# Five small edits to the order and the queues of a one-core, four-part transformer kernel

## The chip, the cores and the metric

The kernel runs on one core of one Trainium2 chip. A core has five engines that each work through their own list of instructions in order: TensorE (PE in the profile, with its weight loads as PEld), VectorE (DVE), ScalarE (ACT), GpSimd (POOL) and SyncE (SP). They meet only at semaphores. Transfers between memories are issued by an engine's queue (here SP's and ACT's, written SPq and ACTq) and carried out by 16 DMA engines. The metric is the device time of one execution in microseconds, as the median of several runs. All data are float32 except some weight codes.

## The reference

Two layers act in turn on an activation `x` of shape (2, 512, 256). Each has an attention and a feed-forward part, and each part is wrapped in two norms:

```python
x = x + layernorm(attn0(layernorm(x)))    # 16 heads of 128, rope, causal softmax, residual inside
x = x + layernorm(ffn0(layernorm(x)))     # gelu(x Wg) * (x Wu), then Wd; weights in 4-bit codes, 2048 wide
x = x + layernorm(attn1(layernorm(x)))    # linear attention: running sums of k and of k*v
x = x + layernorm(ffn1(layernorm(x)))     # silu(x Wg) * (x Wu), then Wd; weights from a 16-entry table, 688 wide

# inside attn0, for each of 2 sequences and 16 heads
q, k = rope(q + bq), rope(k + bk)
attn = softmax(where(causal, -inf, q @ k.T / sqrt(128)))
o    = attn @ v
```

## The kernel before, in words

The 1024 rows of `x` are held in on-chip memory for the whole run, as two sequences of four tiles of 128 rows. The first layer's attention is a loop over 32 "heads" (2 sequences of 16 heads), one call of `slot(i)` for each, with two more calls at the end. The other three parts work on four units `u` of two tiles each.

**The start.** The four tiles of the first sequence come in as four transfers: the two first ones from SP's queue, the two others from ACT's, behind a small transfer of bias columns (`cols_sb`). SP's queue then issues the weights of q and k, the rope tables (`cos_sb`, `sin_sb`), the weights of v, and more. `first_norms(0, 0.0)` computes the statistics of tile after tile on VectorE, the factors on GpSimd, and the normed tiles on ScalarE (tiles 0 and 1) and VectorE (tiles 2 and 3, `centred`). TensorE transposes each tile; ScalarE copies the result with the affine factors into `xT0`, in two halves of two tiles. `project("q", 0)` is done in two halves for that reason. Then come k of head 0, values, and q of head 1.

**A slot.** In `slot(i)` TensorE does, in this order: the scores of head i (4 matrix products), the projections of q and k of head i+1, the output projection of head i-2 (`projected_out`), a values projection where one is due, `attended(i - 1)` (probabilities of head i-1 times values), and later another values projection. In the slots 0 and 1 the values projection stands ahead of `attended`. VectorE takes the score rows out of PSUM with their minimum, ScalarE takes the exponentials and scales them by the inverse sums, and `turned_p(i)` transposes the probabilities: VectorE turns 32 x 32 blocks into the tile `turned`, and four transfers put its four groups of 32 partitions together into `pT`. There is one `turned` and one `pT` (`bufs=1`): `turned_p(i)` can write `turned` only when the transfers of head i-1 have read it, and the transfers can write `pT` only when `attended(i - 1)` has read it. For head 0 alone two of the four transfers are issued by ACT's queue; for all others SP's queue issues the four.

A projection (`project`) is four matrix instructions into one PSUM buffer of a pair (tag `mm`), then for q of a head above 1 three VectorE operations (one into `ra`, two into `rr`) and a GpSimd addition into `qT`; for k of such a head ScalarE and GpSimd take the place of the first of these.

**The norms.** `norms(u, y, stage, to)` ends each of the three first parts for unit u. For both tiles it computes the statistics of `y`, adds the normed `y` to `x`, computes the statistics of the new `x` (`stats` gives `rstd` and `shift`, whose last steps are small GpSimd operations), and lets ScalarE write the normed copy of `x` into a tile `n`. The copy is then turned into the layout that the next part needs: by VectorE and four transfers, or, for the last unit of the last part (stage 3) only, by four TensorE transposes and two ScalarE copies.

**The order.** It is fixed while the program is built. Norms and other side work are generators, and a small planner with a rough cost model decides after which step of TensorE each is continued: `yield until(a, b)` gives the planner's estimate of the time until `a` and `b` are written, and `poll()`, called after every step, continues what is due by the planner's clock. So a `yield` in a generator is a place where its instructions may fall behind others in every engine's list.

**The end.** The last tile of the last unit goes through a shorter path in `written`, and its result is stored as two transfers of 64 rows each, one from SP's queue and one from ACT's. All other output tiles are stored as one transfer of 128 rows from SP's queue.

Most engine operations show the line of a helper (L181 for all of VectorE, ScalarE and GpSimd, L163 for transfers, L272 and L278 for TensorE's products and transposes), so the trace is read by tile names.

Of the kernel before, what the change touches and what calls it, by code (L numbers as in the profile page):

```python
# [19 lines left out]
P = 128  # L20
# [12 lines left out]
HT = 2  # L33
# [155 lines left out]
def sandwich_kernel(  # L189
# [92 lines left out]
    def until(*aps):  # L282

        return max(0.0, times.written(*aps) - now[0])
# [3 lines left out]
    cols_sb = const.tile([P, 3 * NH + 2 * NK], F32, name="cols_sb")  # L288
    scalar.dma_start(out=cols_sb, in_=cols)
    for t in range(NT):  # L290
        (scalar if t >= HT else sync).dma_start(
            out=x0[0][:, t, :], in_=x[0][t * P : (t + 1) * P, :]
        )
    cos_sb = const.tile([P, S], F32, name="cos_sb")
# [47 lines left out]
    def norms(u, y, stage, to, eps=EPS, strided=False):  # L342

        x = [xs[u][:, j, :] for j in range(HT)]
        first = [stats(t, eps) for t in y]
        second = []
        for j in range(HT):
            yield until(first[j][0])  # L350
            add_scaled(x[j], y[j], first[j][0])
            second.append(stats(x[j], EPS))
        yield until(*(t for f in second for t in f))
        n = acts.tile([P, HT, D], F32, tag="ln", name=f"ln{stage}_{u}")


        by_blocks = (u, stage) != (NUNIT - 1, 3)
        for j in range(HT):
            rstd, shift = second[j]
            to_n, from_x = n[:, j, :], x[j]  # L360
            if not by_blocks:
                to_n = to_n.rearrange("p (k f c) -> p k f c", k=NK, c=4)
                from_x = from_x.rearrange(
                    "p (c f k) -> p k f c" if strided else "p (k c f) -> p k f c", k=NK, c=4
                )
            elif strided:
                to_n = to_n.rearrange("p (k m) -> p k m", k=NK)
                from_x = from_x.rearrange("p (m k) -> p k m", k=NK)
            scalar.activation(to_n, from_x, AF.Identity, bias=shift, scale=rstd)
        yield until(n)  # L370
        if by_blocks:

            tr = acts.tile([P, 4, NK, HT, 32], F32, tag="ln", name=f"tr{stage}_{u}")
            for j in range(HT):
                vector.transpose(
                    tr[:, :, :, j, :], n[:, j, :].rearrange("p (k c f) -> p c k f", k=NK, c=4)
                )
            for a in range(4):
                sync.dma_start(
                    out=to[:, a].rearrange("p k j t -> p (k j t)"),  # L380
                    in_=tr[32 * a : 32 * a + 32].rearrange("f c k j t -> f c (k j t)"),
                )
        else:
            pt = bank("t")
            for kc in range(NK):
                for j in range(HT):
                    transpose(
                        pt[:, kc * TU + j * P : kc * TU + (j + 1) * P],
                        n[:, j, kc * P : (kc + 1) * P],
                    )  # L390
            for kc in range(NK):
                scalar.copy(
                    to[:, :, kc].rearrange("p a j t -> p j a t"),
                    pt[:, kc * TU : (kc + 1) * TU].rearrange("p (j a t) -> p j a t", j=HT, a=4),
                )
        for j in range(HT):
            scalar.activation(x[j], x[j], AF.Identity, bias=first[j][1])
        yield until(to)
# [100 lines left out]
    with ExitStack() as at:  # L499
# [54 lines left out]
        def first_norms(b, wait):  # L554
# [138 lines left out]
            out=mask,  # L693
            in_=mask,
# [84 lines left out]
            rs[i] = small.tile([P, NT], F32, tag="rs", name="rs")  # L779
            vector.reciprocal(rs[i], sums[i])  # L780

        def project(kind, i, tag="mm"):
            b, h = divmod(i, NH)
            gg, hh = divmod(i, HG)
            w = wts[kind, gg]
            bias = col(kind, h)
            a = qk.tile([P, S], F32, tag="ra", name="ra")
            r = qk.tile([P, S], F32, tag="rr", name="rr")
            to = qk.tile([P, S], F32, tag=f"T{kind}", name=f"{kind}T")
            lo, hi = slice(0, 64), slice(64, 128)  # L790

            for cs in [slice(0, TU), slice(TU, S)] if (kind, i) == ("q", 0) else [slice(0, S)]:
                ps = bank(tag)
                for kc in range(NK):
                    matmul(
                        ps[:, cs],
                        w[:, kc, hh * DK : (hh + 1) * DK],
                        xT0[b][:, kc, cs],
                        kc == 0,
                        kc == NK - 1,  # L800
                    )
                if (kind == "k") == (i > 1) and i:
                    scalar.activation(a, ps, AF.Identity, bias=bias)
                    pool.tensor_mul(a, a, cos_sb)
                else:
                    vector.scalar_tensor_tensor(
                        a[:, cs], ps[:, cs], bias, cos_sb[:, cs], ALU.add, ALU.mult
                    )
                vector.scalar_tensor_tensor(
                    r[lo, cs], ps[hi, cs], bias[hi], sin_sb[hi, cs], ALU.add, ALU.mult  # L810
                )
                vector.scalar_tensor_tensor(
                    r[hi, cs], ps[lo, cs], bias[lo], sin_sb[lo, cs], ALU.add, ALU.mult
                )
            if (kind, i) == ("k", 1):
                inverted(0)
            (pool if i > 1 or kind == "q" else vector).tensor_add(to, a, r)
            (qT if kind == "q" else kT)[i] = to
# [51 lines left out]
        def turned_p(i):  # L870

            p, _ = ps_p.pop(i)
            for it in reversed(range(NT)):
                n = it + 1
                vector.transpose(
                    turned[:, :, 3 * it : 3 * it + n, :].rearrange("p j t b -> p t j b"),
                    p[:, p_at[it] : p_at[it] + n * P].rearrange("p (t j a) -> p t j a", t=n, j=4),
                )
            pT[i] = pr.tile([P, 4, 13, 32], F32, tag="pT", name="pT", bufs=1)
            for j in range(4):  # L880
                (scalar if i == 0 and j % 2 else sync).dma_start(
                    out=pT[i][:, j].rearrange("p t b -> p (t b)"),
                    in_=turned[32 * j : 32 * j + 32].rearrange("a j t b -> a j (t b)"),
                )
# [107 lines left out]
        def slot(i):  # L992
# [52 lines left out]
            else:  # L1045
                assert not terms
            for kind in "qk":
                if (kind, i) == ("q", 0):
                    pass
                elif i + 1 < NS:  # L1050
                    project(kind, i + 1)
                elif i <= NS:
                    next(main)
                    next(main)
                if kind == "q" and jobs and i % 2 == 0 and i >= 2:
                    dequantised(*jobs.popleft())
                if kind == "q" and i and now_in:
                    inverted(i)
            if now_in:
                p, _ = ps_p[i]  # L1060
# [5 lines left out]
            if i == 0:  # L1066
                values(0, 1, "t")
            elif i == 1:
                values(1, 1, "t")
            if 1 <= i < NS + 1:  # L1070
                attended(i - 1)
            if i == 0:
                values(1, 0)
            if now_in:
                turned_p(i)
            poll()
            if i < NS - HG:
                if i > 1:
# [193 lines left out]
    def written(u, j, y):  # L1272
        x = xs[u][:, j, :]
        row = ((u % 2) * HT + j) * P
        to = out[u // 2][row : row + P]
        if (u, j) != (NUNIT - 1, HT - 1):
            rstd, shift = stats(y, EPS)
            yield until(rstd, shift)
            add_scaled(x, y, rstd)
            vector.tensor_scalar(x, x, shift, None, ALU.add)  # L1280
            sync.dma_start(out=to, in_=x)
            return

        st = small.tile([P, 2, 6], F32, tag="st", name="st_last")
        mv = small.tile([P, 2], F32, tag="mv", name="mv_last")
        for c in range(2):
            vector.bn_stats(st[:, c, :], y[:, c * P : (c + 1) * P])
        vector.bn_aggr(mv, st)
        ve = small.tile([P, 1], F32, tag="ve", name="ve_last")
        vector.tensor_scalar(ve, mv[:, 1:2], EPS, None, ALU.add)  # L1290
        rstd = small.tile([P, 1], F32, tag="rstd", name="rstd_last")
        pool.tensor_tensor(rstd, ve, mhalf[:, :1], ALU.pow)
        centred = acts.tile([P, HT, D], F32, tag="ln", name="centred")[:, 0, :]
        vector.tensor_scalar(centred, y, mv[:, 0:1], None, ALU.subtract)
        add_scaled(x, centred, rstd)
        for engine, rows in ((sync, slice(0, P // 2)), (scalar, slice(P // 2, P))):
            engine.dma_start(out=to[rows], in_=x[rows])

    def run(work, steps=99):
        for _, _ in zip(range(steps), work):  # L1300
# [103 lines left out]
```

## Time and profile before

| What | us |
|---|---|
| Median of three runs (630.89 to 633.00) | 631.77 |
| The profiled execution, by its own time | 631.6 |
| Its span, from the first to the last instruction | 629.8 |
| TensorE busy in the span (98%) | 619.6 |
| VectorE busy (77%) | 487.7 |
| ScalarE busy (47%) | 298.2 |
| GpSimd busy (44%) | 277.8 |
| TensorE waiting for the transfers of `pT` (once) | 1.5 |
| TensorE waiting for tile `n` in the first norm (twice) | 1.3 |
| TensorE waiting for `ln` in the last norm (once) | 0.4 |

The span leaves out 1.8 us of the profiled execution that lie around it. The granted clock of TensorE is 0.998 of full speed. A row of the timeline is: start, duration, engine, line, operation, output and inputs with their sizes, count, and in brackets the engine's idle time before it with what ended it. In the list of waits a row gives who waited for what, then the total, the number of times and the longest. In the chain of work that ended last a row is start, duration, and the work.

### The profile page before, as it was taken

The page shows a single profiled execution, that of the slowest core. Times are in us where ns is not written, and L with a number is a line of the kernel's source. Part 1 is how long each engine was busy: PE and PEld are TensorE (multiplying, and loading weights), DVE is VectorE, ACT ScalarE, POOL GpSimd, SP SyncE. Part 2 cuts the span into 40 slices and gives each one's busy share as a digit, 9 for nine tenths or more (in the row PEclk, how much of TensorE's full clock was granted, in tenths as well). Part 3 has the DMA queues.
Part 4 walks back from the last instruction along what each step waited for, and adds up shares of the span by engine and source line. Part 5 has one row for each costly group of instructions (what it writes and reads, how often), then busy time and mean ns, then how long its engine had stood idle before and what let it go on. Part 6 is the DMA issues. An engine that isn't in the chain of part 4 may idle for free.

```text
span 629.8 us, 8201 instructions
## 1 busy us (share of the span) xinstructions
PE 619.6 (98%) x2504; PEld 461.7 (73%) x2504; DVE 487.7 (77%) x1154; ACT 298.2 (47%) x654; POOL 277.8 (44%) x350
## 2 busy tenths in 40 slices
PE   8999999999999999999999999999999999999996
PEld 5556666666666666666666778888888888888885
DVE  6869889878777989999988989779976372384843
ACT  4655666666655566656655661232313404415130
POOL 4254667546355375575666410350261151163341
PEclk9999999999999999999999999999999999999999
DMA  7366465474565656557453422211001001001000
GB/s 251 89 166 174 136 167 164 99 198 122 117 180 130 156 151 148 151 141 200 109 132 82 95 55 57 101 34 34 1 6 29 1 0 35 0 3 32 26 27 17
DMA packets 42444, 60.07 MB, mean 95 GB/s; under 512 B 5024, under 2 KB 29856, under 8 KB 42400
## 3 DMA queue, kind: packets, MB, share of 16 engines
q1 hardware_dynamic: 41600, 58.76, 35.7%
q10 hardware_dynamic: 800, 0.78, 0.5%
q8 instruction: 20, 0.33, 0.2%
q14 instruction: 24, 0.20, 0.1%
HBM read 28.33 MB, written 1.05 MB: 47 GB/s over the span
## 4 chain that ended last, share of the span: by engine, by line
PE 95%; DMA 2%; DVE 1%; issue 0%; ACT 0%; POOL 0%; ACTq 0%; POOLq 0%
PE ps_mm L272 38%; PE ps_o L272 22%; PE ps_s L272 21%; PE ps_t L272 14%; DMA pT<-turned 1%; DMA x<-in_x 1%; PE ps_t L278 0%; DVE turned L181 0%; DVE rr L181 0%; ACT ln L181 0%; POOL rstd L181 0%; ACTq L163 0%; DVE st L181 0%; DVE ra L181 0%; ACT p L181 0%
## 5 line engine op out<-in xcount | busy, mean ns | idle before, releaser
L181 POOL TENSOR_TENSOR wg<-wg,scratch 128x752 f32<-128x752 f32 x30 | 53.8, 1794 | 98.0 <-DVE scratch L181 98.0
L181 DVE SCALAR_TENSOR_TENSOR rr<-ps_mm,cols_sb,sin_sb 64x512 f32<-64x512 f32 (+1 forms) x126 | 93.4, 741 | 2.6 <-ACT ra L181 0.2
L181 ACT ACTIVATE p<-p,mn 128x512 f32<-128x512 f32 (+3 forms) x128 | 70.6, 552 | 31.3 <-DVE mn L181 31.3
L272 PE MATMUL ps_mm<-xT,wg 128*128 128x256 f32 (+1 forms) x352 | 84.9, 379 | 0.0
L272 PE MATMUL ps_s<-xT,wu 128*128 128x256 f32 x336 | 81.0, 379 | 0.0
L272 PE MATMUL ps_o<-wd,hT 128*128 128x256 f32 (+1 forms) x364 | 78.2, 372 | 0.0
L272 PE MATMUL ps_t<-pT,v 128*128 128x512 f32 (+3 forms) x256 | 74.3, 433 | 1.5 <-DMA pT<-turned 1.5
L272 PEld LDWEIGHTS ps_o<-wd,hT 128*128 128x128 f32 x364 | 67.4, 190 | 8.8
L272 PEld LDWEIGHTS ps_mm<-xT,wg 128*128 128x128 f32 (+1 forms) x352 | 66.4, 189 | 9.3 <-ACT ge L181 0.3
L272 PEld LDWEIGHTS ps_s<-xT,wu 128*128 128x128 f32 x336 | 63.8, 190 | 8.7
L272 PEld LDWEIGHTS ps_t<-pT,v 128*128 128x128 f32 x256 | 48.6, 190 | 28.9 <-issue 15.3
L181 DVE CUSTOM_DVE_ANT_0 p<-ps_s,mask 128x512 f32<-128x512 f32 (+2 forms) x96 | 45.9, 510 | 30.0 <-PE ps_s L272 29.9
L181 ACT ACTIVATE p<-p,rs 128x512 f32<-128x512 f32 (+3 forms) x128 | 61.4, 550 | 10.9 <-DVE rs L181 8.8
L272 PEld LDWEIGHTS ps_o<-wo,oT 128*128 128x128 f32 x256 | 48.6, 190 | 19.0 <-issue 13.6
L181 POOL TENSOR_TENSOR qT<-ra,rr 128x512 f32<-128x512 f32 x32 | 40.8, 1277 | 47.1 <-DVE rr L181 47.1
L272 PE MATMUL ps_s<-kT,qT 128*128 128x512 f32 (+2 forms) x192 | 60.9, 452 | 0.1
L272 PE MATMUL ps_o<-wo,oT 128*128 128x256 f32 x256 | 60.5, 379 | 0.0
L272 PE MATMUL ps_mm<-xT,wq 128*128 128x512 f32 (+1 forms) x128 | 58.4, 579 | 0.0
L272 PE MATMUL ps_mm<-xT,wk 128*128 128x512 f32 x124 | 58.3, 592 | 0.0
L272 PEld LDWEIGHTS ps_s<-kT,qT 128*128 128x128 f32 x192 | 36.0, 190 | 26.8 <-issue 15.9
L181 DVE STREAM_TRANSPOSE turned<-p 128x512 f32<-128x512 f32 (+3 forms) x128 | 54.1, 480 | 1.7 <-DMA pT<-turned 0.6
L272 PE MATMUL ps_mm<-wv,xTv 128*128 128x256 f32 x232 | 54.9, 379 | 0.0
(138 smaller groups left out, 912.8 us busy)
## 6 DMA issues: line engine op xcount, KB each, us to landing
pT<-turned SPq DMA_DIRECT2D x126, 208.0 KB, 3.9
wo<-in_wo SPq DMA_DIRECT2D x17, 256.0 KB, 4.0
wq<-in_wq SPq DMA_DIRECT2D x16, 256.0 KB, 4.0
wk<-in_wk SPq DMA_DIRECT2D x16, 256.0 KB, 4.0
wv<-in_wv SPq DMA_DIRECT2D x16, 256.0 KB, 4.1
xT<-tr SPq DMA_DIRECT2D x44, 64.0 KB, 2.2
pk_g<-in_gate_p SPq DMA_DIRECT2D x4, 256.0 KB, 5.0
sc_g<-in_gate_s SPq DMA_DIRECT2D x8, 128.0 KB, 4.4
```

The costliest lines, as they stand in the source:

```text
L181: return write(*args, **more)
L272: nc.tensor.matmul(out, lhsT=lhsT, rhs=rhs, start=start, stop=stop, **more)
```

## The change

It consists of five edits.

1. Tile 3 of the first sequence is loaded by SP's queue and not by ACT's. In SP's list it stands after tiles 0 and 1 and ahead of the weights of q.
2. The projection of q of head 3 is taken out of slot 2. Its four matrix instructions now stand in slot 1, between the values projection and `attended(0)`; its VectorE and GpSimd operations stand in slot 1 after `turned_p(1)`. For that, `project` is split at a `yield` after the matrix instructions; all other projections run through it without a stop.
3. The four transfers of head 0's `pT` are all issued by SP's queue.
4. In `norms`, the single wait of the planner for the factors of both tiles is replaced by one wait per tile, ahead of that tile's copy. This holds for every call of `norms`.
5. The last tile is stored by one transfer of 128 rows from SP's queue.

```diff
     for t in range(NT):
-        (scalar if t >= HT else sync).dma_start(
+        (scalar if t == HT else sync).dma_start(
             out=x0[0][:, t, :], in_=x[0][t * P : (t + 1) * P, :]
         )
...
             second.append(stats(x[j], EPS))
-        yield until(*(t for f in second for t in f))
         n = acts.tile([P, HT, D], F32, tag="ln", name=f"ln{stage}_{u}")
...
         for j in range(HT):
             rstd, shift = second[j]
+            yield until(rstd, shift)
             to_n, from_x = n[:, j, :], x[j]
...
-        def project(kind, i, tag="mm"):
+        def project(*args):
+            for _ in projection(*args):
+                pass
+
+        def projection(kind, i, tag="mm"):
+
             b, h = divmod(i, NH)
...
                         kc == NK - 1,
                     )
+                yield
                 if (kind == "k") == (i > 1) and i:
...
             for j in range(4):
-                (scalar if i == 0 and j % 2 else sync).dma_start(
+                sync.dma_start(
                     out=pT[i][:, j].rearrange("p t b -> p (t b)"),
...
             for kind in "qk":
-                if (kind, i) == ("q", 0):
+                if (kind, i) in (("q", 0), ("q", 2)):
                     pass
...
                 values(1, 1, "t")
+            if i == 1:
+
+                ahead = projection("q", 3)
+                next(ahead)
             if 1 <= i < NS + 1:
                 attended(i - 1)
             if i == 0:
                 values(1, 0)
             if now_in:
                 turned_p(i)
+            if i == 1:
+                next(ahead, None)
             poll()
...
-        for engine, rows in ((sync, slice(0, P // 2)), (scalar, slice(P // 2, P))):
-            engine.dma_start(out=to[rows], in_=x[rows])
+        sync.dma_start(out=to, in_=x)
```

## The prediction, made before the changed kernel was run

> **What bounds the kernel now.** I read the page's chain of work that ended last, then TensorE's waits, then the timeline where these waits lie.
>
> ```profile
> PE 95%; DMA 2%; DVE 1%; issue 0%; ACT 0%; POOL 0%; ACTq 0%; POOLq 0%
> ```
>
> TensorE carries 95% of the chain: between about 33 and 603 us one product follows the next. A change can pay only at the two ends and in TensorE's few waits:
>
> ```profile
> PE ps_t L272 <- DMA pT<-turned: 1.5, 1, 1.5
> PE ps_o L536 <- POOL ident masks.py:199: 1.4, 1, 1.4
> PE ps_t L278 <- DVE n L181: 1.3, 2, 0.9
> PE ps_t L278 <- ACT ln L181: 0.4, 1, 0.4
> ```
>
> The first row is the `pT` wait in slot 1; the third lies in the first norm and the last in the last norm (the second precedes the first load). At the start:
>
> ```profile
> 1.17 0.93 ACTq L163 DMA_DIRECT2D x<-in_x  x2
> ...
> 1.63 0.43 SPq L163 DMA_DIRECT2D wq<-in_wq  x1
> ...
> 6.56 0.43 DVE L181 BATCH_NORM_STATS2 st<-x 128x6 f32<-128x256 f32 x1 [1.22 <-DMA x<-in_x]
> ...
> 8.62 0.44 PE L278 MATMUL ps_t<-ident,n 128*128 128x128 f32 x2 [0.41 <-DVE n L181]
> ...
> 9.10 1.02 ACT L181 ACTIVATE xT<-ps_t,cols_sb 128x256 f32<-128x256 f32 x2 [1.17 <-PE ps_t L278]
> ...
> 10.71 1.88 PE L272 MATMUL ps_o<-xT,wk 128*128 128x512 f32 x4
> ```
>
> ScalarE's queue issues tiles 2 and 3 at 1.17 and 1.64. VectorE, free since 5.33, sits idle for 1.22 until tile 3 is there; the trace's landing records put it at 6.53, while tiles 0, 1 and 2 landed at 3.00, 3.74 and 3.97. The second half of the `xT` copies (9.10), and with it q's second half and k (10.71), follow. The first `pT`, then the second:
>
> ```profile
> 25.27 1.31 SPq L163 DMA_DIRECT2D pT<-turned  x2
> 25.28 2.22 ACTq L163 DMA_DIRECT2D pT<-turned  x2
> ```
>
> ```profile
> 32.54 2.39 PE L272 MATMUL ps_t<-pT,v 128*128 128x512 f32 x8 [1.49 <-DMA pT<-turned]
> ...
> 34.96 3.35 SPq L163 DMA_DIRECT2D pT<-turned  x4
> ...
> 42.09 2.32 PE L272 MATMUL ps_t<-pT,v 128*128 128x512 f32 x8
> ```
>
> The four transfers of head 0 landed at 28.84, 31.23 (SP), 30.99 and 32.40 (ACT), so 7.13 after the first issue; TensorE, done with values at 31.05, starts `attended(0)` at 32.54. The four of head 1 are issued at 34.96, as that product ends, because there is one `pT`; they landed by 41.66, 6.70 later. In the next three slots the span is 6.5 to 6.7. `attended(1)` starts at 42.25 in the chain: only 0.6 after its data. In the last norm and at the end:
>
> ```profile
> 602.18 0.36 POOL L181 TENSOR_SCALAR shift<-mv,rstd 128x1 f32<-128x1 f32 x1
> ...
> 603.38 0.64 ACT L181 ACTIVATE si<-ps_mm 128x256 f32<-128x256 f32 x2 [2.86 <-PE ps_mm L272]
> 603.60 0.27 POOL L181 TENSOR_SCALAR shift<-mv,rstd 128x1 f32<-128x1 f32 x1
> ...
> 603.93 1.55 ACT L181 ACTIVATE ln<-x,shift,rstd 128x256 f32<-128x256 f32 x2
> ...
> 605.53 0.55 PE L278 MATMUL ps_t<-ident,ln 128*128 128x128 f32 x3 [0.35 <-ACT ln L181]
> ```
>
> ```profile
> 624.28 2.73 SPq L163 DMA_DIRECT2D out<-x  x2
> ...
> 626.45 0.59 ACTq L163 DMA_DIRECT2D out<-x  x1
> ```
>
> Tile 0's factors are ready at about 602.5, tile 1's at 603.87; both copies run behind the `si` pair, and TensorE waits for the second. The halves of the last store landed at 628.50 (SP) and 628.74 (ACT), 1.06 before the span's end.
>
> **What the Trainium skill says.** "DMA: Bandwidth & Descriptors", section "Queues, rings and completion order": an engine takes turns between the queues packet by packet, and serves one queue in order. The trace agrees: tile 3, second on ACT's queue with rows of 1 KB, landed 0.28 after q's weights (6.25; rows of 2 KB), which were issued on the other queue at the same time. The same page, "Rules for kernel authors": splitting a transfer into partition halves isn't worth it, and two queues save issue time alone. The trace agrees here too: the seven whole stores took 1.7 to 2.0 from issue to landing where the landing is separable, the halves 2.05 and 2.29, with issues of 0.57 and 0.59 where a whole one takes 0.33.
>
> **The change, part by part.**
>
> *Tile 3 on SP.* It is issued at about 1.6 as before, but ahead of q's weights. Bounds for its landing: 3.97 (tile 2) and 6.53. I estimate 4.4: tiles 1 and 2, 256 KB, came 0.97 apart from tile 0, so 128 KB is about 0.5. Only by 5.25 does VectorE want it. Then statistics, aggregate and `ve` take 0.83 as for tile 2 (4.51 to 5.33), ending at 6.08; GpSimd's `rstd` (0.55) follows that of tile 2, which ends at 6.25: 6.80; the normed tile runs 6.83 to 7.24 instead of 8.15 to 8.56; the transposes end at 7.74, not 9.06. That would be 1.32. But ScalarE copies the first half of `xT` until 7.93, so the second starts at 7.95 instead of 9.10: **1.15**. From there to the scores at 16.13 TensorE has no gap, and VectorE's chain (first `ra` at 9.96) moves by at least as much, so the scores start at 14.98. Cost: SP's later issues slip by one of 0.43, q's and k's weights, the rope tables and v among them. With that added in full, q's weights land at 6.68 (needed at 7.6), the cosines at 8.10 (needed at 8.6), the sines at 8.77 (needed at 9.1). The cover is thin for the tables, but these are limited by bytes ahead of them, which don't change. Ends for this edit: 0 and 1.3.
>
> *First `pT` on one queue.* Moved by 1.15, the first issue is at 24.12. At 6.70 as for head 1, `pT` is complete at 30.8 instead of 31.25. On ACT, 2.22 of issue go away and the exponentials of head 1 start earlier, but its inverse sums come from VectorE behind `rr` (30.02), so this moves nothing.
>
> *q of head 3 a slot early.* Values end at 29.90; four products of 0.43 fill until 31.63; `pT` has been there since 30.8, so the wait is gone and `attended(0)` runs 31.63 to 33.79 (2.16). In slot 2 the same 1.73 go away between `attended(0)` and `attended(1)`: 42.25 − 34.93 = 7.32 become 5.59. **Here the saved time meets a new wait.** The one `pT` lets SP issue head 1's transfers at 33.82, and they are complete at 40.52; TensorE arrives at 39.38 and waits until 40.66 (0.14 from landing to start, as before). With 2.39 for a product after a stall it ends at 43.05 instead of 44.41: 1.36 in all, so these two edits add **0.2** to the 1.15. If the transfers took 6.0, it would be 0.7 more; if 7.1, 0.4 less. The first `pT` could come 0.8 later without harm. The evictions of q3 on VectorE (0.75 + 1.51) fall into its gap of 1.6 before head 2's scores and overrun by some tenths, which are covered by the wait. GpSimd's addition (1.27) is due long before head 3's scores. SP's loads of slot 2 move with `pT`. In later slots `pT` has 1.8 of slack (51.46 against 53.29), so all of the 1.36 stays.
>
> *Copies by tile.* By the planner's rules tile 0's copy is now emitted ahead of the last `si` pair, tile 1's behind it; only the order is taken from it. Then ScalarE does one copy (0.6 to 0.8) after 603.93, ends by 604.7, and TensorE, at 605.07 done with its eight products, does not wait: its 0.35 and some filling go, **0.45**. If the transposes are emitted a step earlier (two products pairs, 0.86), TensorE waits for them instead and up to 0.45 is lost. The other calls of `norms` have no TensorE wait to save. There a copy can hold ScalarE earlier in front of a `ge` or `si`; the price of that is a rival below.
>
> *One store.* It lands 1.7 after 626.45, against 2.29: **0.59**; ends 0 and 0.6.
>
> Sum: 1.15 + 0.21 + 0.45 + 0.59 = 2.4. Against the profiled execution's 631.6 that is 629.2; the median lies 0.17 above it: **629.4**, or 0.38% less.
>
> **The rivals.**
>
> *Tile 3 isn't earlier* (0.15). Two of the 16 engines lag at this time: tile 3's third-last share landed at 5.61, the last at 6.53, so the lag may be the cause and not the queue. For it: q's weights show the same lag (5.42 and 6.25). Against it: tiles 1 and 2, landed by 3.97, show none. The gain is then 0.2 + 0.45 + 0.59, time 630.5.
>
> *The transposes come a step early* (0.12). 629.4 + 0.9 = 630.3.
>
> *No new wait* (0.08). If head 1's transfers take 5.5 or less, TensorE loses nothing in slot 2: 628.1. Against it: no `pT` in the first slots took under 6.5.
>
> *ScalarE is held in front of the `ge` copies* (0.05). The waits show ScalarE's `ln` held for `shift` 11 times, the longest 4.86 (413.3), without a stall of TensorE. In the gate and up products a `ge` may be late by three blocks of 1.73 less its own 0.60, so 4.6. A copy emitted one block earlier is held up to 4.86 + 1.73 = 6.6: a stall of 2.0. It decides from the second stall; with one in each of three units and 6.0 in all the kernel is slower, 635.4. Against it: the `ln` copies near `ge` were held 3.4 at most (519.7).
>
> **How the numbers follow.** The forecast holds 0.60. A measurement of this kernel can tell about 0.3%, or 1.9 us, from no change: faster means under 629.9. The forecast's own spread (the ends of the `pT` span and of tile 3, and the runs' own 630.9 to 633.0) puts about a fifth of it above that line; of the first two rivals a quarter falls below it. Together: faster 0.62, same 0.32, slower 0.06. The range is 628.1, where no new wait comes, to 631.2, where tile 3 and the transposes both fail.
>
> **What would show it.** Right: no DMA wait ahead of VectorE's fourth statistics; scores of head 0 at about 15.0; `attended(0)` without a wait, and a wait of about 1.3 on `pT` at 40.7 in its place; scores of head 3 about 1.4 earlier than 46.14; the last `ln` pair split around `si`, and no wait of TensorE for it; 1.7 from the last issue to landing. Wrong: a wait of TensorE anywhere between 45 and 600 us, tile 3 landing after 5.3, or a `pT` of head 1 that is complete before TensorE asks for it.

## The result, and the profile after

The changed kernel takes 629.14 us (median of 5 runs, 628.93 to 629.59) against 631.77 (630.89 to 633.02, 5 runs). The ratio is 0.9954 with a 95% interval of 0.9939 to 0.9970. The profiled execution takes 629.14, with a span of 627.3 instead of 629.8.

First the chain that ended last, by engine, and all waits of TensorE, as before:

```profile
PE 96%; DMA 1%; POOL 1%; issue 0%; DVE 0%; SPq 0%; POOLq 0%
```

```profile
PE ps_o L536 <- POOL ident masks.py:199: 1.4, 1, 1.4
PE ps_t L272 <- DMA pT<-turned: 1.3, 1, 1.3
```

Of the three waits that the kernel before had after its first load, those of the first and the last norm are gone. One for `pT` is left, almost as long as before (1.3 against 1.5), but it is another one. The timeline at the start:

```profile
0.72 1.33 SPq L163 DMA_DIRECT2D x<-in_x  x3
...
1.16 0.45 ACTq L163 DMA_DIRECT2D x<-in_x  x1
...
5.36 0.42 DVE L181 BATCH_NORM_STATS2 st<-x 128x6 f32<-128x256 f32 x1
...
7.01 1.93 ACT L181 ACTIVATE xT<-ps_t,cols_sb 128x256 f32<-128x256 f32 x4 [0.53 <-PE ps_t L278]
...
9.53 1.88 PE L272 MATMUL ps_o<-xT,wk 128*128 128x512 f32 x4
...
14.99 1.96 PE L272 MATMUL ps_s<-kT,qT 128*128 128x512 f32 x6
```

The scores of head 0 stood in the kernel before at

```profile
16.13 1.96 PE L272 MATMUL ps_s<-kT,qT 128*128 128x512 f32 x6
```

VectorE's fourth statistics (5.36) no longer wait for a transfer: by the landing records tile 3 is there at 4.78 instead of 6.53. All four `xT` copies run as one block from 7.01, k follows at 9.53 instead of 10.71, and the scores of head 0 start at 14.99. Slots 0 to 2:

```profile
24.13 12.96 SPq L163 DMA_DIRECT2D pT<-turned  x8
...
29.74 1.88 PE L272 MATMUL ps_mm<-xT,wq 128*128 128x512 f32 x4
...
31.46 2.32 PE L272 MATMUL ps_t<-pT,v 128*128 128x512 f32 x8
...
40.73 2.39 PE L272 MATMUL ps_t<-pT,v 128*128 128x512 f32 x8 [1.34 <-DMA pT<-turned]
```

SP issues the first two `pT` (one row, eight transfers). TensorE fills the old stall with q of head 3 (29.74) and starts the product of head 0 without a wait, but stands still 1.34 before that of head 1 (40.73). The last norm and the last stores:

```profile
600.88 0.36 POOL L181 TENSOR_SCALAR shift<-mv,rstd 128x1 f32<-128x1 f32 x1
...
601.27 0.83 ACT L181 ACTIVATE ln<-x,shift,rstd 128x256 f32<-128x256 f32 x1 [2.05 <-POOL shift L181]
...
602.14 0.65 ACT L181 ACTIVATE si<-ps_mm 128x256 f32<-128x256 f32 x2
602.30 0.27 POOL L181 TENSOR_SCALAR shift<-mv,rstd 128x1 f32<-128x1 f32 x1
...
602.68 0.83 ACT L181 ACTIVATE ln<-x,shift,rstd 128x256 f32<-128x256 f32 x1
...
603.60 0.60 PE L278 MATMUL ps_t<-ident,ln 128*128 128x128 f32 x4
```

```profile
622.40 2.50 SPq L163 DMA_DIRECT2D out<-x  x2
```

The first `ln` copy has moved ahead of the `si` pair, only the second runs behind it, and the four transposes run as one block without a wait. The last store is issued at 624.57 and landed 1.69 later, where the later half took 2.29.

So the difference of the spans, 2.49, divides at points that both traces have. In us:

| Stretch | before | after | difference |
|---|---|---|---|
| start to scores of head 0 | 16.13 | 14.99 | -1.14 |
| from there to the scores of head 3 | 29.85 | 29.70 | -0.15 |
| from there to the last unit's output projection | 548.57 | 548.55 | -0.02 |
| from there to the end of the last transposes | 11.53 | 10.96 | -0.57 |
| from there to the issue of the last store | 20.37 | 20.37 | 0.00 |
| from there to its landing | 2.29 | 1.69 | -0.60 |

### The profile page after: what moved, and what is told of

Read it like the earlier page. It is cut to its first block, busy times and chain, and to the rows that moved or that the text cites. A ratio compares the mean times of both kernels' runs of the same rounds, so it can differ in the third digit from the quotient of the medians.

```text
span 627.3 us, 8200 instructions
## 1 busy us (share of the span) xinstructions
PE 619.3 (99%) x2504; PEld 461.7 (74%) x2504; DVE 486.5 (78%) x1154; ACT 298.1 (48%) x654; POOL 276.8 (44%) x350
## 4 chain that ended last, share of the span: by engine, by line
PE 96%; DMA 1%; POOL 1%; issue 0%; DVE 0%; SPq 0%; POOLq 0%
PE ps_mm L272 39%; PE ps_o L272 22%; PE ps_s L272 21%; PE ps_t L272 14%; DMA pT<-turned 1%; POOL rstd L181 0%; DMA x<-in_x 0%; SPq L163 0%; PE ps_t L278 0%; DVE st L181 0%; POOL shift L181 0%; POOLq L1411 0%; DVE x L181 0%; DVE n L181 0%; DVE mv L181 0%
```

## The experiments

The first six take one edit alone, or leave one out. They are read by the stretches of this table, since whole runs of one kernel differ by 1 us and more. The last four stretches agree to 0.02 between kernels that share the edits made there. The first two move by themselves: where nothing in it was changed, the second took 29.71 to 30.04 in six traces, as TensorE's wait for the first `pT` came out shorter or longer. A difference of 0.1 in it shows nothing.

**Tile 3 alone.**

```diff
# before
-        (scalar if t >= HT else sync).dma_start(
+        (scalar if t == HT else sync).dma_start(
```

> The kernel before with the first edit alone (tile 3 on SP's queue). Theory (turns between two queues held the tile back): tile 3 lands by about 4.8 us, VectorE's fourth statistics don't wait, the scores of head 0 start at 15.0 instead of 16.13, and everything after is 1.15 us earlier, span 628.7. Rival (two slow DMA engines, or the other edits, made the tile early): it lands after 6 us and the span stays within 0.3 us of 629.8.

```profile
15.08 1.96 PE L272 MATMUL ps_s<-kT,qT 128*128 128x512 f32 x6
```

Measured: tile 3 landed at 4.49, the scores start at 15.08, the span is 628.8. The theory holds for the trace. The median is 630.54 (14 runs) against 631.08 (41 runs), ratio 0.9987 (0.9979 to 0.9996): half of what the profile promised. Across the traces of all kernels that keep the tile on ACT's queue it landed between 5.83 and 6.54, and the scores start between 15.4 and 16.1 (those with the halved clock told of below apart), so the profile of the kernel before is at the late end. The 41 runs fall into two groups: 31 lie at 632.05 or below, with a median of 630.92, 0.4 above this kernel's; the other ten lie about 2 to 3 above it. Of the experiments' traces from this chip one has the tile on ACT's queue and an undisturbed clock, that of q of head 3 alone: there the tile landed at 5.83 and the scores start at 15.42, 0.34 later than here. Which start the other runs had, no trace shows.

**One queue for the first `pT`.**

```diff
# before
-                (scalar if i == 0 and j % 2 else sync).dma_start(
+                sync.dma_start(
```

> The kernel before with the third edit alone (head 0's four transfers of pT on SP's queue). Theory (a queue of its own only shares the same engines): the four are complete 6.7 us after the first issue instead of 7.13, the product of head 0 starts 0.4 us earlier, span 629.4; ScalarE's exponentials of head 1 start 1.6 us earlier and this moves nothing. Rival (two queues carry more at once): complete after 7.13 us or later, TensorE's wait grows, span 629.8 or more.

Measured: complete 6.81 after the first issue; head 1's exponentials start 1.7 earlier in relation to the first issue (0.60 after it instead of 2.27), and from the scores of head 0 to those of head 3 it takes 29.55 instead of 29.85. So about 0.3 comes of it. Over the six traces of kernels with this edit, head 0's transfers take 6.7 to 6.9, over seven without it 6.5 to 7.3: mostly longer, but not always. The ratio is 0.9990 (0.9981 to 0.9999). Its span, 630.6, was longer for a reason that has nothing to do with `pT`. The table of stretches shows it, in the column PEclk:

```profile
core 0: us, PE busy (x) PEld busy (x) DVE busy (x) ACT busy (x) POOL busy (x), PEclk, DMA share, GB/s
0.00:8.60 8.60, 5.78 (x28) 5.07 (x29) 5.14 (x15) 3.71 (x6) 3.98 (x14) 1.00 0.79 259
8.60:12.20 3.60, 3.60 (x11) 2.85 (x10) 1.50 (x4) 2.15 (x3) 1.59 (x2) 0.53 0.89 320
```

TensorE's granted clock is halved for 3.41 us (from 8.71 to 12.12, by the clock's own records), which it isn't in the profile of the kernel before. The scores start at 17.18. More on this below.

**q of head 3 alone, and everything but that.**

```diff
# q3 alone: before, with projection() split, and
-                if (kind, i) == ("q", 0):
+                if (kind, i) in (("q", 0), ("q", 2)):
...
+            if i == 1:
+                ahead = projection("q", 3)
+                next(ahead)
             if 1 <= i < NS + 1:
                 attended(i - 1)
...
             if now_in:
                 turned_p(i)
+            if i == 1:
+                next(ahead, None)
# all but q3: the changed kernel with these lines as they were
```

> The kernel before with the second edit alone (q of head 3 in slot 1). Theory (one pT buffer: the saved wait comes back a slot later): no wait at the product of head 0, which starts at 32.8; head 1's transfers are issued as it ends at 34.95, and TensorE waits about 1.2 us for them, the product of head 1 ending at 44.2 instead of 44.41; span 629.6. Rival (the filled stall is kept): no wait in slot 2, the product of head 1 ends at 42.9, span 628.3.

> The changed kernel without the second edit (q of head 3 back in slot 2). Theory: the product of head 0 waits for pT, which is complete at 30.8, and ends at 33.3; slot 2 has 7.32 us of work until the product of head 1, which waits for nothing and ends at 42.8, about 0.3 us earlier than in the changed kernel (43.12); span 627.0. Rival (the edit is worth its 1.3 us): the product of head 1 ends at 44.4, span 628.6.

TensorE in slots 1 and 2, with q of head 3 alone, and then without it:

```profile
30.18 1.88 PE L272 MATMUL ps_mm<-xT,wq 128*128 128x512 f32 x4
...
31.90 2.32 PE L272 MATMUL ps_t<-pT,v 128*128 128x512 f32 x8
...
41.20 2.39 PE L272 MATMUL ps_t<-pT,v 128*128 128x512 f32 x8 [1.38 <-DMA pT<-turned]
```

```profile
31.11 2.40 PE L272 MATMUL ps_t<-pT,v 128*128 128x512 f32 x8 [1.24 <-DMA pT<-turned]
...
33.53 3.26 SPq L163 DMA_DIRECT2D pT<-turned  x4
...
40.66 2.32 PE L272 MATMUL ps_t<-pT,v 128*128 128x512 f32 x8
```

Alone, the edit takes the wait away from the product of head 0 and puts one of 1.38 ahead of that of head 1. Without it the wait of 1.24 stands at the first, and none at the second, although the transfers were issued at 33.53, as the first product ended. From the scores of head 0 to those of head 3: 29.85 before, 29.74 with this edit alone, 29.60 with all but this edit, 29.70 with all. These differences are within what the stretch does by itself, so neither a gain nor a loss of the edit is shown in either kernel. What is shown is the step of the theory that matters: the wait moves to the next product and nearly keeps its size. The times agree: ratio 0.9995 (0.9983 to 1.0008) alone, and 0.9957 (0.9941 to 0.9973) without it, as good as the whole change.

**Copies by tile alone.**

```diff
# before
-        yield until(*(t for f in second for t in f))
...
             rstd, shift = second[j]
+            yield until(rstd, shift)
```

> The kernel before with the fourth edit alone (a planner's wait per tile in norms). Theory: until the last unit's last norm nothing on TensorE moves (transposes of the last norm reached at the same time as before, within 0.1 us); there the copy of tile 0 runs ahead of the si pair, TensorE doesn't wait, and all that follows is 0.5 us earlier; span 629.3. Rival (the reordered copies help or hinder along the whole second half): the difference is there already at the last unit's output projection (594.55 before), or TensorE shows new waits for ScalarE.

TensorE's waits:

```profile
PE ps_o L536 <- POOL ident masks.py:199: 1.4, 1, 1.4
PE ps_t L272 <- DMA pT<-turned: 1.3, 1, 1.3
PE ps_t L278 <- DVE n L181: 1.3, 2, 0.9
PE ps_t L278 <- ACT n L181: 0.4, 2, 0.2
```

The row with `ln` is gone. From the scores of head 3 to the last unit's output projection the trace has 548.55 (before 548.57), from there to the end of the transposes 10.97 (11.53). So the gain of 0.56 shows in the last norm alone, and the other calls of `norms` neither help nor hinder. The absolute times, among them a span of 630.2, are 1 us late, as the clock was halved at the start here too. Ratio 0.9980 (0.9967 to 0.9993). That is 1.3 us, and more than the edit's 0.56: of the 31 runs of the kernel before that it is taken against, 16 lie above 632.4 and have the lower mean clock. The same holds for the ratio of the next experiment.

**The store: one transfer, and both halves on one queue.**

```diff
# one transfer: before
-        for engine, rows in ((sync, slice(0, P // 2)), (scalar, slice(P // 2, P))):
-            engine.dma_start(out=to[rows], in_=x[rows])
+        sync.dma_start(out=to, in_=x)
# both halves on SP: before
-        for engine, rows in ((sync, slice(0, P // 2)), (scalar, slice(P // 2, P))):
+        for engine, rows in ((sync, slice(0, P // 2)), (sync, slice(P // 2, P))):
```

> The kernel before with the fifth edit alone (the last tile stored in one transfer). Theory: issue at 626.45 as before, landing after 1.7 us instead of 2.29, span 629.2. Rival (the end is set by something else, such as the engines' own last steps): the landing is earlier and the span stays at 629.8.

> The kernel before with both halves of the last store on SP's queue. Theory (two queues that issue at the same instant hold each other up: 0.57 and 0.59 instead of 0.33): issues of 0.33 one after the other, each half landing 1.7 after its own issue, the last about 2.05 after the first issue instead of 2.29. Rival (half a tile is slower in itself): a half still takes 2.05 or more from its own issue.

SP's last issues, one transfer and then two halves:

```profile
626.42 0.33 SPq L163 DMA_DIRECT2D out<-x  x1
```

```profile
626.31 1.20 SPq L163 DMA_DIRECT2D out<-x  x2
```

One transfer: issue 0.33, landing 1.70 after it, span 629.2, ratio 0.9981 (0.9969 to 0.9994). Two halves on one queue: issues at 626.31 and 626.93 of 0.56 and 0.59, landing 2.01 and 2.05 after their own issue, the last one 2.67 after the first. My theory, that the two queues held each other up, is wrong for the issues, which are as long on one queue. For the landing it is right in part: issued at the same instant on two queues, the second half to land took 2.29 or 2.30 in all six traces, and here 2.05. But each half takes longer than a whole tile (0.33 and 1.7) even so. Why, no run shows.

**A place of its own for head 0's `pT`, and values ahead of the product.** If the new wait is what keeps q of head 3 from paying, removing the cause or filling the gap must free it.

```diff
# two places: the changed kernel
+        both = fw.tile([P, 4, UNIT], F32, name="wd_23")
...
-            w = fw.tile([P, 2, UNIT], F32, name=f"wd{u}")
+            w = fw.tile([P, 2, UNIT], F32, name=f"wd{u}") if u < 2 else both[:, 2 * u - 4 : 2 * u - 2, :]
...
-            pT[i] = pr.tile([P, 4, 13, 32], F32, tag="pT", name="pT", bufs=1)
+            if i == 0:
+                flat = both.rearrange("p a b -> p (a b)")[:, : 4 * 13 * 32]
+                pT[i] = flat.rearrange("p (j t b) -> p j t b", j=4, t=13)
+            else:
+                pT[i] = pr.tile([P, 4, 13, 32], F32, tag="pT", name="pT", bufs=1)
# values first: the changed kernel
             elif i == 1:
                 values(1, 1, "t")
+            elif i == 2:
+                values(2, 0)
...
-                if i > 1:
+                if i > 2:
                     values(i // 2 + 1, odd)
```

> The changed kernel with a place of its own for head 0's pT (in the space of two later weight tiles of the first feed-forward part, which become one tile), so that head 1's transfers need not wait for the product of head 0. Theory (the one buffer makes the new wait): they are issued at 32.7, as VectorE's turned blocks end, instead of 33.81, are complete at 39.4, and the product of head 1 starts at 39.5 instead of 40.73 and ends at 41.8; span 626.0. Rival (the transfers themselves or the single tile of turned blocks set the time): issue or landing stay where they are, span 627.3.

> The changed kernel with the values projection of slot 2 ahead of the product of head 1 instead of behind it. Theory (the new wait can be filled in turn): TensorE does the 1.73 us of values from 39.4 to 41.1, then the product of head 1 without a wait until 43.3; the scores of head 3 start at 43.3 instead of 44.85, nothing waits in slot 3, span 625.8. Rival (the wait moves on once more): TensorE waits for pT in slot 3, since its transfers start as late as before, and less than half of the 1.5 us is kept.

The timeline with two places, and with values first:

```profile
32.61 3.31 SPq L163 DMA_DIRECT2D pT<-turned  x4
...
39.47 2.39 PE L272 MATMUL ps_t<-pT,v 128*128 128x512 f32 x8 [0.21 <-DMA pT<-turned]
```

```profile
39.33 1.89 PE L272 MATMUL ps_mm<-wv,xTv 128*128 128x256 f32 x8
...
41.06 2.32 PE L272 MATMUL ps_t<-pT,v 128*128 128x512 f32 x8
...
43.22 1.89 PE L272 MATMUL ps_s<-kT,qT 128*128 128x512 f32 x6
```

With two places, head 1's transfers are issued at 32.61, when the turned blocks are done, and the wait shrinks to 0.21. From the scores of head 0 to those of head 3 it takes 28.56, against 29.70 in the changed kernel. The span is 626.1, the ratio 0.9944 (0.9923 to 0.9964), the median 627.99. That shows the cause: what the transfers wait for was changed, and they and the product followed. (The two weight tiles that lend the space became one; the later stretches are as before, 548.57 among them.) With values first, TensorE does them from 39.33 and then the product of head 1 without a wait; no wait is left in the whole trace after the first load. The span is 625.9, the median 627.49 (4 runs), the ratio 0.9935 (0.9918 to 0.9953). All four runs lie below every run of both kernels, and no further memory is needed. The same stretch takes 28.12, in which TensorE is busy throughout; the 29.70 of the changed kernel are 28.36 busy and the wait of 1.34. Values first without the edit of q was not run; there the wait of 1.24 stands ahead of the first product.

**The place in the line, and the gap.** Two more on the start.

```diff
# behind q: the changed kernel
-    for t in range(NT):
+    for t in range(NT - 1):
...
         load("q", 0)
+        sync.dma_start(out=x0[0][:, NT - 1, :], in_=x[0][(NT - 1) * P : NT * P, :])
         load("k", 0)
# busy: before, in the transposes of first_norms
                     if t == 0:
                         warm_up(1)
+                    elif t == 1:
+                        warm_up(4)
+                    elif t == 2:
+                        warm_up(2)
```

> The changed kernel with tile 3 still on SP's queue but behind the weights of q of heads 0 and 1. Theory (its place in the line decides, not which engine issues it): it lands at 5.5 to 6.8 with or after q's weights, VectorE waits for it, the scores of head 0 start at 15.5 to 16.2, the span is 0.5 to 1.2 us longer than that of the changed kernel, and executions with the halved clock come back. Rival (leaving ACT's queue is enough): it lands by 5.1 and the scores start at 15.0.

> The kernel before with six more warm-up products on TensorE (identity times identity, result unused): four between the transposes of tiles 1 and 2, two between those of tiles 2 and 3, so that it is not idle while tile 3 is late. Theory (its idle gap there is what lets the clock drop to half for 3.4 us in some executions): tile 3 lands as late as before, at 5.8 to 6.5, but no execution has the lower mean clock of 0.996 and a time above 632.3; median 630.9. Rival (the drop has nothing to do with that gap): a quarter to a half of the executions lie above 632.3 as for the kernel before.

VectorE's statistics of tile 3 behind q's weights, and TensorE's added products in the other:

```profile
6.13 0.43 DVE L181 BATCH_NORM_STATS2 st<-x 128x6 f32<-128x256 f32 x1 [0.75 <-DMA x<-in_x]
```

```profile
6.97 1.21 PE L536 MATMUL ps_o<-ident 128*128 128x128 f32 x8
...
8.23 0.61 PE L536 MATMUL ps_o<-ident 128*128 128x128 f32 x4
```

Behind q's weights (landed at 5.77), tile 3 lands at 6.10, though it is on SP's queue: VectorE waits 0.75, the scores start at 15.69, the span is 628.0. So the place in the line decides, and leaving ACT's queue is not enough. The median of 7 runs is 629.32 and none of them had the halved clock, which I had expected to return; with seven runs that is open. (The tile stands behind the weights that serve heads 0 and 1; they are one transfer.)

The other one is about the halved clock. Among 91 runs of the kernel before on three chips, 33 lie above 632.4, with a mean clock of 0.997 or less; the rest lie between 629.99 and 632.3. Of the 38 runs of kernels with tile 3 on SP's queue, none is more than 1.5 above the fastest of its kernel. With six products more in TensorE's gaps, tile 3 landed as late as ever (6.54, scores at 16.12), but of 13 runs none had a mean clock of 0.996 or less, where 7 of 19 runs of the kernel before on the same chip did. Two lay above 632.3 (632.55 and 632.58, at 0.998 and 0.997), against the letter of the expectation. The second may have had the halved clock: the two traces that show it have a mean of 0.997 too. Median 631.57 against 631.81, ratio 0.9994 (0.9980 to 1.0007).

## Why the prediction was right, and where not

The forecast was 629.4, and 629.14 was measured. By its own steps:

- *Tile 3 on SP.* 1.15 was worked out, 1.14 measured, with the scores at 14.99 (14.98), and the bound by ScalarE's copies, not by the tile, as argued: the tile came at 4.78 and not at 4.4, and the copies still run as a block. The tables came in time (cosines 7.77, sines 8.47), 0.10 and 0.13 later than before where up to 0.43 was allowed for. Of the rival with two lagging engines, little is left: with the tile on ACT's queue its last share of 16 landed 0.92 after the third-last in one trace (6.53 and 5.61) and 0.03 after it in another (6.47 and 6.44), and late in both. So the lag is there in some executions, but it is not what makes the tile late; ahead of the weights on SP's queue the two are at most 0.14 apart and both there by 5.14.
- *First `pT` and q of head 3.* 0.21 together was forecast, 0.15 measured; with a stretch that moves by 0.3, this nearness is luck. The mechanism is not: the new wait was forecast at 40.66 with 1.28, and came at 40.73 with 1.34. This is the step that matters: by counting the filled stall alone, 1.3 us more would have been promised. Two experiments then freed 1.14 and 1.58.
- *Copies by tile.* The order of the copies was as worked out, and the transposes follow the same products as before, so the rival of an early step did not come. The size was too small: 0.57 instead of 0.45. The sum counted the idle 0.35 and some filling; but the second transpose had started 0.62 after the first, and now each starts 0.11 after the one ahead.
- *One store.* 0.59 against 0.60.
- *ScalarE held in front of `ge`*, the rival that ended slower: no wait of TensorE anywhere between 45 and 600, and 548.55 for a stretch of 548.57.

The upper end of the range has a slip: a late tile (630.5) and early transposes (0.9 more) make 631.4 and not 631.2. Nothing hangs on it.

What the prediction did not see is that the start of the kernel before differs from one execution to the next. It set its sum against one execution with a late tile, whose scores start at 16.13; others start at 15.42, or at 17.2 with the halved clock. From trace to trace the sum held, 2.4 against 2.49. But in the experiment on tile 3 most runs of the kernel before lie only 0.4 above the edit's median, and ten of 41 lie 2 to 3 above it; as none of the 38 runs with the tile on SP's queue shows such a time, the edit seems to take these away too. The measured 2.63 of the medians contains both, and its nearness to 2.4 is in part luck.

## What to carry to other kernels

When a stall is filled with work from later, look at what the stalled instruction releases: if a buffer is freed by its end, the same chain starts no earlier and the wait comes back where the work was taken from. Move the work that stands behind the next wait along with it, or give the chain a second buffer. Two more are worth trying elsewhere: here a first tile that everything waited for gained by standing ahead of the weights in the same line, and the transfer that ends the kernel by not being cut in halves.

## What the runs showed that I had not expected

**The clock.** In some executions TensorE's clock is halved for 3.41 us, in the two traces that show it from 8.71 (first `pT` on one queue) and from 8.31 (copies alone). The Trainium skill, "TensorE: Matmul & The Clock Gate", "Part 1: The HAM clock gate (the "warmup" mystery)", tells of a monitor with a free-running window of 3.4 us that halves the clock after an idle one. The length agrees. But TensorE was not idle here: in the 3.41 us just before, it was busy 1.97 and 1.95.

The other traces can be set beside these. In each, the clock records begin with the full clock somewhere between 4.5 and 7.3 us, just where TensorE's small products shorten from 0.42 to 0.27; in these two the halving comes 3.41 after that point. In the same 3.41 us of the eleven traces without it, TensorE was busy 2.02 (the kernel before) to 3.41 (the added products), with tile 3 ahead of the weights 2.61 or more. So the two least busy of the thirteen are the two that were followed by the halving. The price was 1.1 at the scores (17.2 instead of 16.1). With only 0.05 between 1.97 and 2.02, that the share busy is what decides is likely and not shown, and no limit can be read from two cases.

**The half store.** A store of 64 rows took 0.56 to 0.59 to issue and 2.00 to 2.30 to land; one of 128 rows of the same 1 KB took 0.33 and mostly 1.7. The Trainium skill, "DMA: Bandwidth & Descriptors", "Rules for kernel authors", advises against halves because they share the engines. The later of two halves issued at once agrees with that (2.29 or 2.30, and 2.05 where it was issued 0.62 behind the other), but each half was slower than a whole tile besides.
